# Routing of a mixture-of-experts layer: pair counting and the router's bias moved to TensorE, one put per four tiles, rows combined two tiles ahead

## The chip, the cores and the metric

The kernel runs on one core of a Trainium2 chip. The metric is the device time of one execution in microseconds (us). In the text PE is TensorE (matrix products), PEld its weight loads, DVE is VectorE, ACT is ScalarE, POOL is GpSimd and SP is SyncE, which issues most DMAs. The chip's memory blocks are SBUF (working memory of 128 partitions) and PSUM (where PE writes).

## The reference, cut to what matters

The program is four layers in a row, each adding to `x` (2048 tokens of 512 numbers: 16 tiles of 128 tokens). The change concerns layer 1, a mixture of 32 experts with 4 chosen for each token:

```python
x = x + _L1_ffn_ref(_L1_cond_ref(x, subject, cond_weights), ...)

def _L1_cond_ref(x, subjects, weights):
    w = weights[subjects]
    return jnp.einsum('bct,bcd->bdt', x, w)

def _L1_ffn_ref(hidden_states, gate_w, gate_b, w_gate, b_gate, w_up, b_up, w_down, b_down):
    E, K = 32, 4
    x = hidden_states.reshape(-1, Hh)
    logits = x @ gate_w.T + gate_b
    topk_logits, topk_idx = jax.lax.top_k(logits, K)
    topk_weight = jax.nn.softmax(topk_logits, axis=-1)
    flat_idx = topk_idx.reshape(-1)
    xs = jnp.repeat(x, K, axis=0)
    order = jnp.argsort(flat_idx)          # tokens sorted by expert
    xt = xs[order]
    ...                                    # gate, up, SwiGLU, down: one product per expert
    outs = outs[inv].reshape(-1, K, Hh)
    return jnp.sum(outs * topk_weight[..., None], axis=1)
```

## The kernel before

Each layer is one function. Layer 0 is itself a mixture of experts (7 experts, 2 chosen); its experts' rows lie in a DRAM scratch tensor `ys`, two rows per token. Layer 1 (`layer1`, from L1051) begins by adding these rows to the token stream and choosing its own experts. That is the stage the change touches. It loops over the 16 tiles of 128 tokens, and for tile `i`:

- `combined` (L980 and on, the add on L988): for each of the two choices of layer 0, POOL issues an indirect DMA (a gather, L284) of 128 rows of `ys` into a buffer `yk` (four buffers), and DVE multiplies them with the gate and adds them to the tile: two adds per tile, the second one completes `x`. Its result is kept in `xk` (named `x1in` in the profile).
- `mm` (L1074): PE multiplies with the conditioning weights; ACT copies the result to `c` (L1076, three buffers); SP writes `c` to the DRAM tensor `rows` (L1077).
- `tp` (L1080): PE transposes `c` in four pieces; ACT copies to `cT` (L1082).
- `rp` (L1085): four PE products with the router's weights; DVE adds the bias, giving `lg` (L1087).
- `choose` (L748, in the profile L751 and L752): DVE takes the eight highest of 32 logits and their indices.

After a group of tiles `put` (L754) gives each token-and-expert pair a slot in a table sorted by expert. It is called with groups of 4, 4, 4, 2, 1 and 1 tiles, each one tile behind the choice:

- `chosen` (L758) and `hot` (L761): the indices become a one-hot array of tiles x 4 choices x 32 experts, in f32.
- `sel` (L766) sums the four choices; `pre` (L768) keeps a running sum over tiles, one add per tile.
- `at` (L771, L772): PE multiplies a matrix of ones with `pre` (pairs in earlier tiles, plus the expert's first slot) and a strictly upper triangular matrix with `sel` (pairs of earlier tokens in the tile). The sum is each token's next slot for each expert.
- the product of `hot` and `at` (L773) and its sum `sl` (L775) pick the slot of each pair; six small DVE steps (L777 to L780, L728 to L733) split it in tile and row.
- `mark` (from L723): DVE builds two one-hot arrays `b` and `a` (L737), ACT scales `a` with the token's number (L743), and PE multiplies them (L745) into a table of token numbers by slot, which DVE adds to `tokens` (L746).

`end` (L783) turns `tokens` into the integer list `stok` (L785). The next stage starts with gathers of `rows` by `stok` (`xr`, L284), transposes (L909) and the experts' products (L928, L947).

The loop is written tile by tile, but a scheduler orders each engine's instructions when the kernel is built; each engine then works through its own list in order. What the program says first decides what the scheduler may place early.

Of the kernel before, what the change touches and what calls it, by code (L numbers as in the profile page):

```python
# [9 lines left out]
F32 = mybir.dt.float32  # L10
BF16 = mybir.dt.bfloat16
# [4 lines left out]
ALU = mybir.AluOpType  # L16
AX = mybir.AxisListType
# [3 lines left out]
P = 128  # L21
B, T, D = 32, 64, 512
NT = B * T // P
# [6 lines left out]
E1, K1, C1, V1 = 32, 4, 320, 56  # L30
UNIT = 320
BIG = 65536.0
W0, W1R = 3072, 3076
# [647 lines left out]
class Moe:  # L681
# [4 lines left out]

    def __init__(self, g, ctx, keep, E, K, C, V, wname, wlen, act, scale):
        self.g, self.keep, self.E, self.K, self.C, self.V = g, keep, E, K, C, V  # L690
        self.wname, self.wlen, self.act, self.scale = wname, wlen, act, scale
        tc = g.tc
        self.tiles = E * C // P
        self.rows = g.stream(f"rows{E}")
        self.ys = g.ys[E]
        self.slot = g.const.tile([P, NT, K], I32, name=f"slot{E}")
        self.gates = g.const.tile([P, NT, K], F32, name=f"gates{E}")
        self.vals = keep.tile([P, NT, 8], F32, name=f"vals{E}")
        self.chosen = keep.tile([P, NT, K], F32, name=f"chosen{E}")
        self.place = keep.tile([P, NT, K], F32, name=f"place{E}")  # L700
        self.idx = keep.tile([P, NT, 8], U32, name=f"idx{E}")

        self.pre = keep.tile([P, NT + 1, E], F32, name=f"pre{E}")
        self.count = keep.tile([P, E], F32, name=f"count{E}")
        self.stok = keep.tile([P, self.tiles], I32, name=f"stok{E}")
        self.wp = ctx.enter_context(tc.tile_pool(name=f"ew{E}", bufs=3, reuse_waits="tile"))
        self.wts = {}
# [8 lines left out]
    def begin(self, sb, bank, at):  # L716
        nc, iota = self.g.nc, self.g.c("iota")[:, 0 : self.E]
        self.bank, self.at = bank, at
        nc.vector.tensor_scalar(self.pre[:, 0], iota, self.C / P, None, ALU.mult)
        self.tok = sb.tile([P, self.tiles], F32, name="tokens", bufs=1)  # L720
        nc.vector.memset(self.tok, 0.0)

# [31 lines left out]
    def put(self, sb, i, n):  # L754

        g, nc, E, K, C = self.g, self.g.nc, self.E, self.K, self.C
        fi, place = self.chosen[:, i : i + n, :], self.place[:, i : i + n, :]
        nc.vector.tensor_copy(fi, self.idx[:, i : i + n, 0:K])  # L758
        shape = [P, n, K, E]
        hot = sb.tile(shape, F32, name=f"hot{n}", bufs=1)  # L760
        nc.vector.tensor_tensor(  # L761
            hot, g.c("iota")[:, 0:E].unsqueeze(1).unsqueeze(1).to_broadcast(shape),
            fi.unsqueeze(3).to_broadcast(shape), ALU.is_equal,
        )
        sel = sb.tile([P, n, E], F32, name=f"sel{n}")
        nc.vector.tensor_reduce(sel, hot.rearrange("p n k e -> p n e k"), AX.X, ALU.add)  # L766
        for j in range(n):
            nc.vector.tensor_tensor(self.pre[:, i + j + 1], self.pre[:, i + j], sel[:, j], ALU.add)  # L768

        at = self.at[:, 0 : n * E].rearrange("p (n e) -> p n e", n=n)  # L770
        nc.tensor.matmul(at, g.ones, self.pre[:, i : i + n], start=True, stop=False)  # L771
        nc.tensor.matmul(at, g.c("upper"), sel, start=False, stop=True)  # L772
        nc.vector.tensor_tensor(hot, hot, at.unsqueeze(2).to_broadcast(shape), ALU.mult)  # L773
        sl = sb.tile([P, n, K], F32, name=f"sl{n}")
        nc.vector.tensor_reduce(sl, hot, AX.X, ALU.add)  # L775
        slot = self.slot[:, i : i + n, :]
        nc.vector.tensor_copy(slot, sl)  # L777
        nc.vector.scalar_tensor_tensor(place, fi, -float(C), sl, ALU.mult, ALU.add)
        ov = sb.tile([P, n, K], F32, name=f"ov{n}")
        nc.vector.tensor_scalar(ov, place, float(C), BIG, ALU.is_ge, ALU.mult)  # L780
        self.mark(sb, self.bank[:, 0 : self.tiles], self.tok, sl, slot, ov, i, n, self.tiles)

    def end(self, sb):  # L783
        g, nc, E, C = self.g, self.g.nc, self.E, self.C
        nc.vector.tensor_copy(self.stok, self.tok)  # L785

        lim = sb.tile([P, E], F32, name="lim")
        nc.vector.tensor_scalar(lim, g.c("iota")[:, 0:E], float(C), float(C), ALU.mult, ALU.add)  # L788
        tot = self.at[:, 0:E]
        nc.tensor.matmul(tot, g.ones, self.pre[:, NT], start=True, stop=True)  # L790
        nc.vector.tensor_tensor(self.count, tot, lim, ALU.subtract)
        nc.vector.tensor_scalar(self.count, self.count, 0.0, None, ALU.max)

# [257 lines left out]
def layer1(g, bridge, combined, beside, w2):  # L1051
    tc, nc, a = g.tc, g.nc, g.a
    with ExitStack() as ctx:
        keep = ctx.enter_context(tc.tile_pool(name="l1keep", bufs=1, reuse_waits="tile"))
# [2 lines left out]

        xk = w2["pool"].tile([P, NT, D], F32, name="x1in", tag="sb_mu")
        bd = g.load(keep, "b_d1")
        m = Moe(g, ctx, keep, E1, K1, C1, V1, "w_e1", W1R, l1_expert, None)  # L1060
        with ExitStack() as c1:
            wp = c1.enter_context(tc.tile_pool(name="l1w", bufs=1, reuse_waits="tile"))
            sb = c1.enter_context(tc.tile_pool(name="l1sb", bufs=3, reuse_waits="tile"))
            ps = c1.enter_context(tc.tile_pool(name="l1ps", bufs=2, space=PSUM, reuse_waits="tile"))
            wr = g.load(wp, "w_r1")
            br = g.load_bcast(wp, "b_r1")
            bank, at = (ps.tile([P, 512], F32, name=k, tag=k, bufs=1) for k in ("tok", "at"))
            m.begin(sb, bank, at)

            groups = {3: 4, 7: 4, 11: 4, 13: 2, 14: 1, 15: 1}  # L1070
            for i in range(NT):
                x = combined(sb, i, 3, bridge.x[i], xk[:, i])
                o = ps.tile([P, D], F32, name="mm", tag="mm")
                nc.tensor.matmul(o, bridge.weights[i], x, start=True, stop=True)  # L1074
                c = sb.tile([P, D], F32, name="c")
                nc.scalar.copy(c, o)  # L1076
                nc.sync.dma_start(out=m.rows[i * P : (i + 1) * P, :], in_=c)  # L1077
                tp = ps.tile([P, 4, P], F32, name="tp", tag="tp")
                for cc in range(4):
                    nc.tensor.transpose(tp[:, cc, :], c[:, cc * P : (cc + 1) * P], g.ident)  # L1080
                cT = sb.tile([P, 4, P], F32, name="cT", bufs=2)
                nc.scalar.copy(cT, tp)  # L1082
                rp = ps.tile([P, E1], F32, name="rp", tag="rp")
                for cc in range(4):
                    nc.tensor.matmul(rp, cT[:, cc, :], wr[:, cc, :], start=cc == 0, stop=cc == 3)  # L1085
                lg = sb.tile([P, E1], F32, name="lg")
                nc.vector.tensor_tensor(lg, rp, br, ALU.add)  # L1087
                m.choose(i, lg)
                for last in (i - 1, i) if i == NT - 1 else (i - 1,):
                    if last in groups:  # L1090
                        m.put(sb, last + 1 - groups[last], groups[last])
# [1049 lines left out]
```

## Time and profile before

| | |
|---|---|
| median of the three runs (lowest to highest) | 2775.95 us (2772.17 to 2790.0) |
| the profiled execution: time, span | 2785.32 us, 2783.5 us |
| mean granted TensorE clock | 0.956 of full |
| busy share of the span: PE, PEld, DVE, ACT, POOL | 93%, 59%, 50%, 27%, 30% |
| first gather of the stage, last add, last choice, slot list written | 636.9, 706.9, 714.6, 725.5 us |
| DVE and PE busy within 636.9 to 725.6 | 63.2 and 60.1 of 88.7 us |

The times of the profile run from the span's start. A row of the timeline gives the start, the duration, the engine, the line, the operation with output and inputs, and in brackets how long the engine had been idle and what released it. A duration of DVE overlaps the next one's start by some 0.08 us, since instructions are pipelined. PE's clock is granted by a throttle, in this stage full in some stretches and half in others.

### The profile page before, as it was taken

How to read it: one execution, taken by the hardware profiler on the slowest of the kernel's cores; microseconds unless marked ns; L12 is line 12 of the kernel's file. 1: busy time of each engine (PE TensorE's matmuls, PEld its weight loads, DVE VectorE, ACT ScalarE, POOL GpSimd, SP SyncE). 2: the span in 40 equal slices, each digit the busy share in tenths (PEclk: the TensorE clock that was granted, in tenths of full speed). 3: DMA queues.
4: the chain of work that ended last, by engine and by line, in shares of the span. 5: the costliest groups of instructions: out<-in, count | busy, mean ns of one | idle time of the engine just before them, and what ended most of it. 6: DMA issues, size and time to landing. Idle time of an engine off the chain costs nothing.

```text
span 2783.5 us, 42018 instructions
## 1 busy us (share of the span) xinstructions
PE 2575.4 (93%) x16556; PEld 1641.2 (59%) x16571; DVE 1401.2 (50%) x3479; ACT 749.3 (27%) x1557; POOL 846.4 (30%) x904
## 2 busy tenths in 40 slices
PE   7999979996799999979899999999999999787778
PEld 5777756654455655646666666766666654344444
DVE  4666655735653333335554444555444326465556
ACT  2444421112211121111222222222322212444444
POOL 2222225504212223212222222222222028654550
PEclk9999999997799999998999999999999999888889
DMA  2333224446456865533000000110001034233330
GB/s 95 128 127 128 85 95 155 157 142 193 153 191 238 313 233 190 197 131 113 27 28 27 28 27 31 46 32 27 27 27 50 9 113 145 66 95 89 98 98 29
DMA packets 107076, 291.20 MB, mean 105 GB/s; under 512 B 20681, under 2 KB 21481, under 8 KB 99568
## 3 DMA queue, kind: packets, MB, share of 16 engines
q1 hardware_dynamic: 71232, 193.46, 19.4%
q0 software_dynamic: 35056, 89.13, 10.7%
q10 hardware_dynamic: 576, 5.77, 0.5%
q8 instruction: 135, 2.21, 0.3%
q14 instruction: 77, 0.63, 0.1%
HBM read 216.76 MB, written 87.56 MB: 109 GB/s over the span
## 4 chain that ended last, share of the span: by engine, by line
PE 49%; DVE 2%; issue 2%; another core or an unknown queue 1%; DMA 1%; ACT 1%; POOL 0%; SPq 0%; ACTq 0%; POOLq 0%; DVEq 0%
PE lp L1374 8%; PE out L1517 8%; PE zp L1451 8%; PE pp L1831 3%; PE hp L1483 3%; PE gp L1506 2%; PE y L2078 2%; PE sp L2009 2%; PE yp L1319 2%; PE op L2056 2%; PE pT L2031 2%; PE ep L1460 1%; PE kp L1982 1%; PE ap L1307 1%
## 5 line engine op out<-in xcount | busy, mean ns | idle before, releaser
L928 PE MATMUL gu<-xT,wt 128*128 128x320 f32 x1472 | 407.1, 434 | 0.0
L928 PEld LDWEIGHTS gu<-xT,wt 128*128 128x128 f32 x1472 | 277.6, 191 | 119.5 <-issue 11.3
L1374 PEld LDWEIGHTS lp<-xnT,sb_mu 128*128 128x128 f32 x2048 | 236.3, 194 | 8.6 <-issue 6.7
L1374 PE MATMUL lp<-xnT,sb_mu 128*128 128x128 f32 x2048 | 239.3, 277 | 1.5 <-DVE xnT L256 0.8
L947 PE MATMUL y<-wt,hT 128*128 128x512 f32 (+1 forms) x552 | 238.7, 606 | 0.6 <-DVE yo L256 0.6
L1517 PE MATMUL out<-sb_w,gT 128*128 128x512 f32 x512 | 233.9, 599 | 0.0
L1451 PE MATMUL zp<-sb_w,xnT 128*128 128x512 f32 x512 | 226.5, 592 | 0.0
L1510 DVE COPY gT<-gp 128x512 f32<-128x512 f32 x64 | 44.2, 691 | 235.4 <-PE gp L1506 235.1
L284 POOL DMA_INDIRECT xr<-rows,stok x115 | 110.0, 957 | 154.1 <-PE tp L909 85.3
L1451 PEld LDWEIGHTS zp<-sb_w,xnT 128*128 128x128 f32 x512 | 93.7, 190 | 104.7 <-issue 100.9
L1517 PEld LDWEIGHTS out<-sb_w,gT 128*128 128x128 f32 x512 | 93.5, 190 | 103.8 <-issue 95.4
L947 PEld LDWEIGHTS y<-wt,hT 128*128 128x128 f32 (+1 forms) x552 | 80.0, 171 | 105.5 <-issue 88.4
L677 POOL TENSOR_TENSOR ga<-ga,sg 128x320 f32<-128x320 f32 x64 | 55.2, 862 | 284.2 <-ACT sg L673 283.4
L284 POOL DMA_INDIRECT yk<-ys,slot x96 | 99.0, 1032 | 125.7 <-DVE lim L788 65.4
L2016 DVE CUSTOM_DVE_ANT_0 s<-sp,mask 128x336 f32<-128x336 f32 x128 | 61.2, 503 | 138.5 <-PE sp L2009 40.0
L1528 POOL TENSOR_TENSOR xt<-xt,bc_bias 128x512 f32<-128x512 f32 x16 | 20.3, 1267 | 359.9 <-DMA x<-xt 359.9
L1488 ACT ACTIVATE h<-hp 128x512 f32<-128x512 f32 x128 | 69.5, 594 | 214.2 <-PE hp L1483 214.1
L284 POOL DMA_INDIRECT kvt<-kv,gidx x96 | 93.5, 974 | 107.0 <-PE op L2056 81.9
L1412 POOL TENSOR_TENSOR eT<-eT,inv 128x512 f32<-128x512 f32 x64 | 71.6, 1119 | 152.2 <-DVE inv L1411 151.2
L284 POOL DMA_INDIRECT kvt<-newkv,oidx x96 | 96.5, 1005 | 33.1 <-issue 29.2
L2078 PE MATMUL y<-sb_w_o,oT 128*128 128x512 f32 x128 | 75.8, 677 | 20.3 <-ACT oT L2059 9.2
L2020 ACT ACTIVATE s<-s,m 128x336 f32<-128x336 f32 x128 | 72.9, 572 | 74.5 <-DVE m L2016 53.3
(388 smaller groups left out, 4601.0 us busy)
## 6 DMA issues: line engine op xcount, KB each, us to landing
wt<-w_e SPq DMA_DIRECT2D x32, 1538.0 KB
ys<-yo SPq DMA_DIRECT2D x115, 256.0 KB
ys<-zero SPq DMA_DIRECT2D x10, 2048.0 KB
xt<-x SPq DMA_DIRECT2D x62, 256.0 KB
wt<-w_e SPq DMA_DIRECT2D x7, 1536.0 KB
x<-xt SPq DMA_DIRECT2D x32, 256.0 KB
sb_w<-w SPq DMA_DIRECT2D x5, 1024.0 KB
rows<-hn SPq DMA_DIRECT2D x16, 256.0 KB
```

What stands on the lines that cost most here:

```text
L284: ins = self.nc.gpsimd.indirect_dma_start(out=out, out_offset=None, in_=src, in_offset=bass.IndirectOffsetOnAxis(ap=idx, axis=0), **kw)
L928: nc.tensor.matmul(o, wj[:, c, ic * P : (ic + 1) * P], xT[:, c, :], start=c == 0, stop=c == 3)
L947: nc.tensor.matmul(y[row : row + n, :], hTs[u][:, ic, col : col + n], wd[:, ic, :], start=ic == 0, stop=ic == 1,)
L1374: g.first(e + c, nc.tensor.matmul(lp[:, e, :], w["mu"][:, c, (4 * q + e) * P : (4 * q + e + 1) * P], self.xnT[:, c, :], start=c == 0, stop ...
L1412: g.pin(nc.gpsimd.tensor_tensor(e3, e3, inv.unsqueeze(2).to_broadcast([P, 8, T]), ALU.mult))
L1451: g.first(c, nc.tensor.matmul(zp, self.xnT[:, c, :], w["w1"][:, c, cols], start=c == 0, stop=c == 3))
L1483: g.first(e + b, nc.tensor.matmul(hp[:, b, e, :], self.ews[q][r, e, :], self.z[q][r, e * P : (e + 1) * P], start=True, stop=True))
L1488: g.pin(nc.scalar.activation(self.hs[q][b], hp[:, b], AF.Gelu))
L1517: g.first(e, nc.tensor.matmul(self.out, self.gTs[q][:, e, :], w["w2"][:, 4 * q + e, :], start=q + e == 0, stop=q + e == 6 and q == 3))
L1831: nc.tensor.matmul(pp, xT[i][:, c, :], (w["w_kv3"] if z else wq)[:, c, :], start=c == 0, stop=c == 3)
L2020: nc.scalar.activation(p, p, AF.Exp, bias=m, scale=-1.0, accum_out=tot)
L2078: nc.tensor.matmul(yp, self.oT[i][:, c // 2, c % 2, :], w["w_o3"][:, c, :], start=c == 0, stop=c == 3)
```

## The change

Layer 1's routing object gets a flag `counts`. With it:

- `hot` is written in bf16. `sel` and `pre` are gone. A running count `base` (32 numbers, the same in each partition) starts as each expert's first slot.
- PE adds up the slots in PSUM: `base` through the identity matrix into `n + 1` blocks of 32 columns, then for each of the four choices the upper triangular matrix times `hot` (4 products), then for each tile and choice the matrix of ones times `hot` into all later blocks (16 products). Block `n` holds the count after the group; ACT copies it to `base`.
- The product goes to an array of its own, `own`, in f32. `end` reads the totals from `base`.
- The router's bias is a fifth PE product into `rp` (one row of ones times the bias), and `choose` reads `rp` in PSUM. `lg` is gone, and the bias is loaded as one row.
- `put` is called for groups 4, 4, 4, 4.
- Tile `i + 2` is combined before tile `i` is multiplied (three tiles before the first).

```diff
+        self.base = keep.tile([P, E], F32, name=f"base{E}") if counts else None
+        self.masks = keep.tile([P, 2, P], BF16, name=f"masks{E}") if counts else None
...
+        if self.base is not None:
+            nc.vector.tensor_scalar(self.base, iota, float(self.C), None, ALU.mult)
+            for j, k in enumerate(("upper", "ones")):
+                nc.vector.tensor_copy(self.masks[:, j], self.g.c(k))
...
-        hot = sb.tile(shape, F32, name=f"hot{n}", bufs=1)
+        hot = sb.tile(shape, BF16 if self.base is not None else F32, name=f"hot{n}", bufs=1)
...
+        own = hot
+        if self.base is None:
...
+        else:
+            own = sb.tile(shape, F32, name=f"own{n}", bufs=1)
+            every = self.at[:, 0 : (n + 1) * E].rearrange("p (n e) -> p n e", n=n + 1)
+            at = every[:, 0:n]
+            nc.tensor.matmul(
+                every, g.ident, self.base.unsqueeze(1).to_broadcast([P, n + 1, E]), start=True, stop=False
+            )
+            for k in range(K):
+                nc.tensor.matmul(at, self.masks[:, 0], hot[:, :, k], start=False, stop=False)
+            for j in range(n):
+                for k in range(K):
+                    nc.tensor.matmul(
+                        every[:, j + 1 :], self.masks[:, 1], hot[:, j : j + 1, k].to_broadcast([P, n - j, E]),
+                        start=False, stop=j == n - 1 and k == K - 1,
+                    )
+            nc.scalar.copy(self.base, every[:, n])
+        nc.vector.tensor_tensor(own, hot, at.unsqueeze(2).to_broadcast(shape), ALU.mult)
...
-        nc.vector.tensor_reduce(sl, hot, AX.X, ALU.add)
+        nc.vector.tensor_reduce(sl, own, AX.X, ALU.add)
...
-            br = g.load_bcast(wp, "b_r1")
+            br = g.load(wp, "b_r1")
...
-            groups = {3: 4, 7: 4, 11: 4, 13: 2, 14: 1, 15: 1}
+            groups = {3: 4, 7: 4, 11: 4, 15: 4}
             for i in range(NT):
-                x = combined(sb, i, 3, bridge.x[i], xk[:, i])
+                for j in range(3) if i == 0 else (i + 2,):
+                    if j < NT:
+                        combined(sb, j, 3, bridge.x[j], xk[:, j])
+                x = xk[:, i]
...
-                    nc.tensor.matmul(rp, cT[:, cc, :], wr[:, cc, :], start=cc == 0, stop=cc == 3)
-                lg = sb.tile([P, E1], F32, name="lg")
-                nc.vector.tensor_tensor(lg, rp, br, ALU.add)
-                m.choose(i, lg)
+                    nc.tensor.matmul(rp, cT[:, cc, :], wr[:, cc, :], start=cc == 0, stop=False)
+                nc.tensor.matmul(rp, g.ones[0:1, :], br, start=False, stop=True)
+                m.choose(i, rp)
```

## Prediction

> **What bounds the kernel now.** I read the cores first (one core, span 2783.5 us, mean clock 0.956; the execution's own time is 2785.32 us), then the table by stretches, to find the stage that the change touches: the first gather of layer 1's rows starts at 636.93 us, and the list of token slots (`stok`) is written at 725.34 us. Nothing before or behind is edited. Columns: stretch, its length, busy time of PE, weight load, DVE, ACT, POOL (instructions in brackets), granted clock, DMA share, GB/s.
>
> ```profile
> 640.00:660.00 20.00, 13.98 (x48) 8.16 (x49) 10.07 (x18) 4.10 (x7) 15.73 (x15) 0.67 0.78 243
> 660.00:680.00 20.00, 16.24 (x87) 11.62 (x85) 12.47 (x57) 6.65 (x12) 10.91 (x11) 0.85 0.69 212
> 680.00:700.00 20.00, 15.93 (x96) 11.28 (x96) 18.89 (x48) 8.30 (x16) 5.63 (x5) 0.83 0.48 155
> 700.00:720.00 20.00, 12.66 (x78) 9.75 (x78) 17.89 (x72) 7.02 (x14) 0.00 (x0) 0.59 0.47 184
> 720.00:740.00 20.00, 10.58 (x43) 7.80 (x44) 11.33 (x50) 2.40 (x5) 10.40 (x11) 0.56 0.59 192
> ```
>
> The reader sees two halves. Up to 660 POOL issues gathers nearly without a pause (15.73 of 20 us) and DVE is half idle; from 680 on DVE is the engine that is never free (18.89 and 17.89 of 20 us), while PE falls to a clock of 0.59. The whole kernel is bound by PE elsewhere (93% busy), but here PE is fed through DVE. The waits of 636 to 726 us say who is late:
>
> ```profile
> DVE x1in L988 <- DMA yk<-ys,slot: 10.3, 9, 4.6
> DVE lg L1087 <- PE mm L1074: 6.8, 2, 4.7
> POOL yk L284 <- DVE vals L751: 10.5, 2, 7.7
> ACT c L1076 <- remote: 7.4, 1, 7.4
> DVE hot L773 <- PE at L772: 1.4, 3, 0.7
> ```
>
> DVE waits for gathered rows only at the start; later the gathers wait for DVE (up to 7.7 us), because a `yk` buffer is freed by an add that stands behind routing work. The two other large waits are one event: between 658.0 and 664.2 us DVE, ACT and PE's next step all stand, for which the busy rows show no work. DVE's timeline gives the three marks that I count with, and POOL's the next stage's start:
>
> ```profile
> 662.67 0.19 DVE L1087 TENSOR_TENSOR lg<-rp,bc_b_r 128x32 f32<-128x32 f32 x1 [4.66 <-PE mm L1074]
> ...
> 706.11 0.75 DVE L988 SCALAR_TENSOR_TENSOR x1in<-yk,gates,x1in 128x512 f32<-128x512 f32 x1
> ...
> 714.41 0.19 DVE L752 FIND_INDEX8 idx<-vals,lg 128x8 uint32<-128x32 f32 x1
> ...
> 725.34 0.20 DVE L785 CAST stok<-tokens 128x80 int32<-128x80 f32 x1
> ```
> ```profile
> 726.28 0.94 POOL L284 DMA_INDIRECT xr<-rows,stok  x1 [32.81 <-DVE stok L785]
> ```
>
> So part A ends with the last add, 706.86. Part B, from there to tile 15's choice (714.60), takes 7.7 us. Part C, from the choice to the slots (725.54), takes 10.9 us. The expert weights are issued at 710.2 and land by 724.2, so they don't end last.
>
> **The change, part by part.** DVE's groups of the stage (busy, mean ns, idle before):
>
> ```profile
> L766 DVE TENSOR_REDUCE sel<-hot 128x128 f32<-128x512 f32 x3 | 3.1, 1028 | 0.0
> L1087 DVE TENSOR_TENSOR lg<-rp,bc_b_r 128x32 f32<-128x32 f32 x16 | 2.9, 184 | 11.1 <-PE mm L1074 6.8 <-PE rp L1085 2.5 <-remote 1.3
> L768 DVE TENSOR_TENSOR pre<-pre,sel 128x32 f32<-128x32 f32 x16 | 2.9, 182 | 0.0
> L737 DVE TENSOR_TENSOR b<-sb_cst,row 128x2048 f16<-128x2048 f32 x3 | 6.8, 2283 | 0.0
> L737 DVE TENSOR_TENSOR a<-sb_cst,tl 128x1280 f16<-128x1280 f32 x3 | 4.4, 1482 | 0.0
> ```
>
> *Removed from DVE.* Instructions overlap by some 0.08 us in the timeline (706.01, 706.11 are a `pre` and the next start), so a group's price is the distance to the next start. Ahead of the last add there are in the old order three wide `sel` (3 x 0.94) and one half-wide (0.58 long, 0.49): 3.3 us; 13 `pre` x 0.10: 1.3; 15 `lg` x 0.10: 1.5. The built program's order moves more behind the last add: the product and reduction for tiles 8 to 11 (0.61 + 0.60), `chosen` and `hot` for 12 and 13 (0.06 + 0.32), two choices (2 x 0.27): 2.1. Together 8.2 us less DVE work in part A. DVE is the busy engine in the last 27 us of A, so I count all of it; if it were hidden by waits for PE it would be worth 0, which is the second rival. The new `base` and `masks` writes (between the 0.18 us of a 32-wide row and the 0.69 of a 512-wide one, each) lie in the 4.56 us in which DVE waits for the first gather. Without that cover the three would cost 0.5 to 2.
>
> *Added on PE.* Each put now needs 20 bf16 pairs between `hot` and the product. No row shows their widths (128 down to 32 columns, mean 90). The nearest is the slot count's f16 pair of 80 columns: 12 in 0.75 us with a last one of 0.20 at full clock, 0.05 each; 8 in 0.72 with a last one of 0.27 at half clock, 0.064. Scaled by 90/80: 1.1 to 1.45 us. The upper bound is the f32 transpose of 128 columns, 0.109 and 0.213 a piece: 2.2 to 4.3. I take the f16 rows, same kind of element. [...] Then ACT copies `base` (the 586 ns copies are of 512 columns; this has 32; 0.3 with hand-over, bounds 0.1 and 0.6), and in the built program the product waits for that copy. In the first three puts the order has adds or choices between `hot` and product, so of about 2 us 1.5 is covered: +0.6 over the 1.4 us that DVE waits there now. The bias takes one f32 matmul (two passes of 0.112 or 0.213) per tile behind the router's four: 0.2 to 0.4 us x 16 on PE, which is 50 of 66 us busy in A: inside the next item.
>
> *Rows two tiles ahead.* POOL's order of gathers is unchanged; what moves is DVE's. In the old order 8 or 9 other adds stand between a tile's second add and its `lg` (tiles 0 and 1); in the new one 5 to 7 stand ahead of its maximum (tiles 0 to 4). So a choice may wait with later adds behind it, and with them the gather buffers and POOL's next gathers. Five adds at the pace of the first 19 gathers (661.64 - 636.93 over 18, 1.37 us) are 6.9 us. A tile's chain is, at full and half clock, matmul 1.1 to 2.0, copy 0.6, transposes 0.6 to 1.1, copy 0.6, router and bias 1.3 to 2.4, hand-overs 0.3: 4.5 to 7.0 us, and tiles queue behind each other on PE. I take +1.0 over the present waits; bounds -2 (the rp waits of 2.5 nearly gone) and +10 (rival two).
>
> A: 706.9 - 8.2 + 0.6 + 1.0 = 700.3.
>
> *B.* New order after the last add: product of 8 to 11, choice 13, reduction, choice 14, the small slot steps, `b`, `a`, and only then choice 15. PE must do the counting pairs, tile 13's router, tile 15's matmul and tile 14's router first. Last add to choice 14: pairs and copy 1.6, router 1.1 to 2.1, matmul 1.0 to 1.7, router and end 1.2 to 2.3: 5.2 to 7.8 (full and half clock, with transposes 0.3). Then small steps 0.8, `b` and `a` 2.20 + 1.48, choice 0.4: 10.1 to 12.7. I take 11.0: +3.3.
>
> *C.* One put of four tiles instead of 2, 1, 1. From the choice: `gates`, `chosen`, `hot` 1.0; 20 pairs with 8 slot matmuls of the put before between them 1.45 + 0.5 + 0.25; `base` 0.3; product 0.7, with two small ones 0.2, reduction 0.7; small steps 0.9; `b` and `a` 3.7; four ACT scalings 1.9 (712.30 in the trace shows them behind `a`); last slot matmuls, sum and cast 1.0. Sum 12.6: +1.7. Of the table load for the exponential (1.28 us) I charge nothing: ACT has it done under `hot` and the pairs; without that cover it delays `base` by up to 1.3. PE stands at 0.50 of its clock in all of 706.9 to 725.6 now, so I price C's pairs at half clock; at full clock they would take 0.35 less. [...]
>
> Sum: -8.2 + 0.6 + 1.0 + 3.3 + 1.7 = -1.6 us. From 2785.32 that is 2783.7 for a profiled execution; the median of the runs shown is 2775.95, 9.4 lower, so 2774.3.
>
> **Rivals.** (1) *DVE's relief shows whole and the gathers set the pace.* 32 gathers at 1.37 us: the last starts at 636.93 + 31 x 1.37 = 679.4, lands 4.0 later, add 0.75: A at 684.2; with B 11.0 and C 12.6 the end is 707.8, -17.7 us: 2758. For: POOL's first 19 go at this pace. Against: the new order binds adds to earlier choices. If also the stand of 658 to 664 went (6.2 us), 2752. (2) *PE's chain replaces DVE, slower.* The place is DVE's queue, where a choice stands ahead of the second add two or three tiles later; it decides once A runs at a clock under 0.6 (now 0.78). At half clock PE needs per tile 1.71 + 4 x 0.21 + 10 x 0.21 = 4.65, 16 of them 74, four puts x 2.1: 83 us from 641, so the last choice comes at 724 to 726, and with C the end is near 738: +12, 2788. For: the half-clock rows of B and C, the smaller lead. Against: PE's own extra work keeps the clock up. (3) *The stand of 658 to 664 us moves with the denser gathers*, 6 us either way, within no change.
>
> **How the numbers follow.** About 1% (27.8 us) is what a measurement of this kernel can tell from no change. The forecast, no change at 2774, has 0.72, with its own range 2764 to 2785; rival one 0.17, of which 0.06 passes 1%; rival two 0.11, of which 0.05 does. Low end: no stand -6.2, waits -3.0, B -0.9, run scatter -4 (lowest run against the median): 2760. High end: waits +9, B +1.7, scatter +4: 2789. Faster 0.06, same 0.89, slower 0.05.
>
> **What would show it.** Right: the last add near 700, choice 15 near 711, `stok` near 724, DVE busy in the stage near 53 us instead of 63.2. Rival one: last add before 690 and no POOL wait over 2 us. Rival two: DVE's largest wait is a maximum for the router's bias, and the clock in 640 to 706 under 0.6. I am wrong if the stage moves by over 15 us, or if time moves outside it.

## The result, and the profile after

The changed kernel takes 2784.12 us (median of 12 runs, 2781.82 to 2789.76), the kernel before 2776.30 (12 runs beside them, 2767.08 to 2790.0). The ratio is 1.0029, 95% interval [1.0015, 1.0043]: slower by about 8 us, where 1.6 us of gain were forecast. The median lies inside the forecast's range of 2760 to 2789, but the move goes the other way.

The profiled execution of the changed kernel has a span of 2786.8 us. Its table by stretches, in the columns of the one shown before (busy time of PE, weight load, DVE, ACT, POOL, then granted clock, DMA share, GB/s):

```profile
640.00:660.00 20.00, 8.85 (x30) 4.78 (x30) 7.64 (x14) 2.34 (x4) 13.67 (x14) 0.65 0.64 180
660.00:680.00 20.00, 17.12 (x89) 12.46 (x88) 8.42 (x24) 5.76 (x10) 11.30 (x12) 0.74 0.69 205
680.00:700.00 20.00, 18.35 (x128) 13.65 (x127) 15.12 (x47) 7.46 (x16) 8.21 (x8) 0.91 0.53 173
700.00:720.00 20.00, 16.71 (x109) 12.33 (x108) 13.54 (x35) 7.00 (x14) 0.96 (x1) 0.80 0.37 116
720.00:740.00 20.00, 6.56 (x60) 5.38 (x59) 13.77 (x44) 5.56 (x11) 3.66 (x4) 0.59 0.57 228
```

This execution reached its first gather at 642.4 us, 5.4 later than the one before (the work ahead of it is not edited; over all profiles that mark lies between 636.9 and 645.2), so the rows are compared by what lies inside the stage. DVE was the engine that was never free (18.89 and 17.89 of 20 us); now it is busy for 15.12 and 13.54, and PE has taken its place with 17.12, 18.35 and 16.71. The marks, from DVE's timeline:

```profile
710.85 0.74 DVE L1017 SCALAR_TENSOR_TENSOR x1in<-yk,gates,x1in 128x512 f32<-128x512 f32 x1
...
721.83 0.19 DVE L759 FIND_INDEX8 idx<-vals,rp 128x8 uint32<-128x32 f32 x1
...
734.48 0.20 DVE L811 CAST stok<-tokens 128x80 int32<-128x80 f32 x1
```

Part A (first gather to the end of the last add) is 69.2 us (before 69.9), part B (to tile 15's choice) 10.4 (7.7), part C (to the slot list) 12.7 (10.9). From the first gather to the first expert product it is 101.6 us against 98.0. So these two executions differ by 3.8 us up to the slot list, and by 3.3 in their spans, while the medians differ by 7.8: the profiled execution of before lies 9 us above its median, that of the change 4.5. No profile here says where the other 4 us lie. What DVE waited for from 636 to 726 us (in total, times, longest):

```profile
DVE x1in L1017 <- DMA yk<-ys,slot: 11.0, 6, 7.0
DVE vals L758 <- remote: 5.8, 1, 5.8
DVE vals L758 <- PE rp L1118: 5.7, 6, 1.5
DVE tokens L753 <- PE tok L752: 3.7, 3, 1.3
DVE own L799 <- ACT base L798: 3.0, 2, 1.9
DVE vals L758 <- issue: 2.7, 1, 2.7
```

L1118 is the new bias product: DVE's choices (`vals`) now wait for PE. The totals of part A, from the busy time of each engine in that stretch, before and after:

```profile
636.90:706.80 69.90, 49.55 (x257) 33.83 (x257) 47.87 (x145) 20.64 (x38) 34.73 (x32) 0.77 0.57 179
```
```profile
642.40:711.60 69.20, 53.35 (x291) 36.92 (x292) 39.98 (x102) 19.80 (x38) 34.10 (x32) 0.77 0.59 176
```

DVE works 47.87 - 39.98 = 7.9 us less in A, and A is only 0.7 us shorter. The mean clock of A is the same, 0.77. Where the other 7.2 us went is the question of the experiments.

### The profile page after: what moved, and what is told of

The parts are those of the page before. It is cut to its first block, busy times and chain, and to the rows that moved or that the text cites. A ratio compares the mean times of both kernels' runs of the same rounds, so it can differ in the third digit from the quotient of the medians.

```text
span 2786.8 us, 42147 instructions
## 1 busy us (share of the span) xinstructions
PE 2583.7 (93%) x16650; PEld 1649.4 (59%) x16665; DVE 1395.6 (50%) x3416; ACT 749.4 (27%) x1561; POOL 844.2 (30%) x904
## 4 chain that ended last, share of the span: by engine, by line
PE 49%; DVE 2%; issue 2%; another core or an unknown queue 1%; DMA 1%; ACT 1%; POOL 0%; POOLq 0%; ACTq 0%; SPq 0%; DVEq 0%
PE lp L1405 8%; PE out L1548 8%; PE zp L1482 8%; PE pp L1862 3%; PE hp L1514 3%; PE gp L1537 2%; PE y L2109 2%; PE sp L2040 2%; PE pT L2062 2%; PE op L2087 2%; PE yp L1350 2%; PE ep L1491 1%; PE kp L2013 1%; PE ap L1338 1%
## 5 line engine op out<-in xcount | busy, mean ns | idle before, releaser
L284 POOL DMA_INDIRECT yk<-ys,slot x96 | 98.1, 1022 | 129.4 <-SPq L845 66.1
L938 PEld LDWEIGHTS tp<-sb_cst,xr 128*128 128x128 f32 x460 | 53.5, 147 | 66.3 <-issue 32.9
```

Of the source, the lines that this page charges most:

```text
L284: ins = self.nc.gpsimd.indirect_dma_start(out=out, out_offset=None, in_=src, in_offset=bass.IndirectOffsetOnAxis(ap=idx, axis=0), **kw)
```

## The experiments

Two kinds of comparison are used. The time is the median and the ratio to the kernel before, run beside it on the same chip. A, B and C are from one profiled execution each. In some sets of runs the kernel before takes about 2680 us, in the others 2771 to 2779 (the record has both for the chip that it numbers 1); in the sets of 2680, A is some 3 to 7 us shorter for the same kernel (66.4 against 69.2 for the changed one), so A is compared among sets of the same level only. "vs before" in us is the median of before times the ratio less one; it need not be the difference of the medians (for "changed, no bias" -6.7 against -2.1).

| kernel | median (before) | ratio [95%] | vs before, us | A, B, C | clock in A |
|---|---|---|---|---|---|
| before, shown / once more | - | - | - | 69.9, 7.7, 10.9 / 69.8, 7.7, 11.0 | 0.77 / 0.74 |
| changed kernel | 2784.12 (2776.30) | 1.0029 [1.0015, 1.0043] | +8.1 | 69.2, 10.4, 12.7 | 0.77 |
| look only | 2681.88 (2679.77) | 1.0005 [0.9993, 1.0017] | +1.3 | 64.9, 6.6, 14.8 | 0.74 |
| counts only | 2677.79 (2679.77) | 0.9991 [0.9983, 1.0000] | -2.4 | 59.7, 10.0, 7.4 | 0.84 |
| bias only | 2691.95 (2679.77) | 1.0048 [1.0034, 1.0062] | +12.9 | 65.4, 14.2, 12.0 | 0.79 |
| groups only | 2682.32 (2679.77) | 1.0003 [0.9991, 1.0015] | +0.8 | 60.5, 6.2, 16.9 | 0.84 |
| bias copied | 2792.05 (2778.83) | 1.0049 [1.0030, 1.0067] | +13.6 | 79.6, 12.1, 12.8 | 0.61 |
| PSUM, no bias | 2786.10 (2778.83) | 1.0032 [1.0013, 1.0052] | +8.9 | 70.1, 12.3, 11.2 | 0.72 |
| changed, bias on DVE | 2773.14 (2778.83) | 0.9984 [0.9966, 1.0002] | -4.4 | 67.9, 10.0, 12.7 | 0.70 |
| changed, no bias | 2769.04 (2771.17) | 0.9976 [0.9961, 0.9992] | -6.7 | 63.8, 9.7, 12.7 | 0.77 |
| changed, ring | 2781.16 (2771.17) | 1.0047 [1.0032, 1.0062] | +13.0 | 62.3, 22.1, 12.0 | 0.76 |
| changed, bias twice | 2774.78 (2771.17) | 1.0011 [0.9995, 1.0028] | +3.0 | 72.9, 10.9, 12.7 | 0.71 |
| counts and look | 2767.93 (2771.17) | 0.9994 [0.9975, 1.0012] | -1.7 | 64.5, 10.8, 9.8 | 0.74 |
| changed, again | 2685.06 (2681.27) | 1.0014 [1.0005, 1.0023] | +3.8 | 66.4, 9.9, 12.7 | 0.72 |
| changed, no bias, again | 2675.77 (2681.27) | 0.9976 [0.9967, 0.9985] | -6.4 | 57.1, 9.8, 12.7 | 0.80 |
| changed, bias in one pass | 2675.01 (2681.27) | 0.9975 [0.9966, 0.9984] | -6.7 | 57.6, 9.6, 12.7 | 0.80 |
| changed, bias twice, again | 2686.49 (2681.27) | 1.0011 [1.0003, 1.0020] | +2.9 | 69.3, 10.8, 12.7 | 0.72 |
| changed, wide scores | 2779.03 (2775.55) | 1.0001 [0.9982, 1.0021] | +0.3 | 60.9, 17.7, 11.7 | 0.78 |
| one pass, wide | 2771.42 (2775.55) | 0.9986 [0.9966, 1.0005] | -3.9 | 59.3, 13.6, 12.6 | 0.81 |

### One part at a time, on the kernel before

Look only: the adds run two tiles ahead. Counts only: the flag `counts`. Bias only: the bias product and the choice from `rp`. Groups only: the last put of four.

```diff
+                for j in range(3) if i == 0 else (i + 2,):          # look only
+                    if j < NT:
+                        combined(sb, j, 3, bridge.x[j], xk[:, j])
...
+        m = Moe(g, ctx, keep, E1, K1, C1, V1, "w_e1", W1R, l1_expert, None, True)   # counts only
...
+                nc.tensor.matmul(rp, g.ones[0:1, :], br, start=False, stop=True)   # bias only
+                m.choose(i, rp)
...
+            groups = {3: 4, 7: 4, 11: 4, 15: 4}                      # groups only
```

> The kernel before with one part of the change: rows combined two tiles ahead. Theory 1 (order): putting each choice closer behind its tile's adds makes DVE wait for PE's chain with later adds behind it; this part alone costs +4 to +10 us. Theory 2 (PE and ACT in DVE's path): the counting on PE with its copy of the base costs the time; this part alone is within -3 to +2 us. Theory 3 (the end of the stage): only the last put of four tiles costs; this part alone within -3 to +2 us.

> The kernel before with one part of the change: pairs counted on PE (bf16 one-hots, base copied by ACT), groups of 4, 4, 4, 2, 1, 1, bias on DVE, rows not ahead. Theory 1: DVE's relief of sel and pre (5 us) shows, -6 to 0 us. Theory 2: the product now waits for 20 matmuls and ACT's copy six times, +3 to +8 us, with DVE's waits for base over 5 us in sum. Theory 3: -5 to 0 us.

> The kernel before with one part of the change: the router's bias as a fifth product into PSUM, the maximum read from PSUM. Theory 1: -3 to +1 us (1.6 us of DVE gone). Theory 2: 0 to +3 us, since each router chain is 0.2 to 0.4 us longer on PE. Theory 3: -3 to +1 us.

> The kernel before with one part of the change: the last four tiles in one put instead of 2, 1, 1. Theory 3: +3 to +6 us, from the last choice to the slot list about 12.5 us instead of 10.9. Theories 1 and 2: 0 to +2 us.

None of the three parts that the theories on record name (the order of the rows, counting, the last put) moves the time by more than 2.4 us. Counting as the cost is excluded by its interval; for the order (up to +4.6 us) and the last put (up to +4.0, with a C of 16.9 where 12.5 was expected) the intervals just reach the low ends of what was expected. The part that none of them named, the bias, costs 12.9 us by itself.

### Which half of the bias part costs: the product, or reading PSUM twice

The kernel before is profiled once more here, for its A, B and C on another chip. In "bias copied" the bias is added on PE and DVE copies the sum out of PSUM at once, so a bank is as short-lived as before. In "PSUM, no bias" the bias is left out and the choice reads PSUM, so the bank is held as in the change. In "changed, bias on DVE" only the bias part of the change is undone.

```diff
-                m.choose(i, rp)                       # bias copied, from bias only
+                lg = sb.tile([P, E1], F32, name="lg")
+                nc.vector.tensor_copy(lg, rp)
+                m.choose(i, lg)
...
-                nc.tensor.matmul(rp, g.ones[0:1, :], br, start=False, stop=True)   # PSUM, no bias
...
-                m.choose(i, rp)                       # changed, bias on DVE
+                lg = sb.tile([P, E1], F32, name="lg")
+                nc.vector.tensor_tensor(lg, rp, br, ALU.add)
+                m.choose(i, lg)
```

> The kernel before itself, profiled on the chip of the experiments (one look). Expected, if the bias part's cost of about 13 us sits in the stage between the first gather of rows and the first expert product: a stage shorter than the 100.8 us of the bias-only kernel by 8 to 13 us, so 88 to 93. If the cost sits elsewhere (layer 2, or the stage of layer 0): a stage of 97 to 101 us, and the rest of the kernel shorter than the 1947.6 us of the bias-only kernel.

> Before with the bias added on TensorE, and the sum then copied from PSUM to SBUF by VectorE, which chooses from the copy: VectorE has as many instructions as before, TensorE has the extra product, and the PSUM bank of a tile's scores is free again after one short copy. Theory 'held bank' (the bias part costs because the choice reads PSUM twice, and the next-but-one tile's router product waits for the second read): no change against before, -3 to +3 us. Theory 'TensorE's extra product' (the K=1 product lengthens the router's chain): as slow as the bias-only kernel, +8 to +13 us.

> Before with no bias added at all (left out: the router's bias), the choice made straight from PSUM: no extra product on TensorE, no add on VectorE, and the bank held through Max and MaxIndex. Theory 'held bank': about as slow as the bias-only kernel, +8 to +13 us. Theory 'TensorE's extra product': faster than before by up to VectorE's 16 adds of 0.2 to 0.3 us, -5 to 0 us.

> The changed kernel with only the bias back on VectorE (added there on the way out of PSUM, as before): counts on TensorE, groups of four, rows combined two tiles ahead. If the bias part alone turned the change into a loss: faster than before by 2 to 8 us, the stage 5 us or more shorter than the changed kernel's 101.6. If the parts only lose together (order and the last put of four): within 2 us of before or slower, stage 98 us or more.

The look at before does not place the cost: its stage is 97.7 us, as in the profile shown (98.0), but the 100.8 us of "bias only" that it was to be held against come from a set of the other level. Of the two theories neither stands alone: both halves cost, each +8.9 us or more. But the order of DVE's instructions in these two kernels also differs from the order before in thirty to forty places, so what the order did is not kept apart. The product's half is seen in "bias copied", first in what DVE waits for, then in the busy time of A (before, once more, below it):

```profile
DVE lg L1117 <- PE rp L1115: 22.9, 10, 6.4
```
```profile
643.90:723.50 79.60, 62.72 (x252) 43.85 (x253) 44.06 (x126) 19.34 (x35) 37.57 (x32) 0.61 0.49 153
```
```profile
645.20:715.00 69.80, 49.11 (x257) 33.37 (x257) 48.13 (x145) 20.61 (x38) 34.05 (x32) 0.74 0.57 179
```

PE is busy for 62.72 us instead of 49.11 and its clock falls from 0.74 to 0.61; A is 9.8 us longer. The other half lies in B. In "PSUM, no bias" A stays (70.1), but tile 15's index (L759) stands behind the wide `b` and `a`, though its maximum was taken at 715.80:

```profile
715.80 0.20 DVE L758 MAX8 vals<-rp 128x8 f32<-128x32 f32 x1 [0.59 <-PE rp L1114]
...
716.70 2.29 DVE L744 TENSOR_TENSOR b<-sb_cst,row 128x2048 f16<-128x2048 f32 x1
718.90 1.48 DVE L744 TENSOR_TENSOR a<-sb_cst,tl 128x1280 f16<-128x1280 f32 x1
...
720.70 0.19 DVE L759 FIND_INDEX8 idx<-vals,rp 128x8 uint32<-128x32 f32 x1
```

So B is 12.3 instead of 7.7: an order that the scheduler built. In the whole change that place was priced in part B of the forecast. With the bias back on DVE the change has a median 5.7 us below before, though its interval just reaches 1. Its second mark was missed: its stage was to be 5 us or more shorter than the changed kernel's 101.6 and is 99.9, longer than the 97.7 of before on the same chip. So this run does not show that the bias alone turned the change into a loss.

### Nothing, one, or twice the product, in the changed kernel

```diff
-                nc.tensor.matmul(rp, g.ones[0:1, :], br, start=False, stop=True)   # no bias: left out
...
+                nc.tensor.matmul(rp, g.ones[0:1, :], br, start=False, stop=False)  # bias twice: one more
...
-                rp = ps.tile([P, E1], F32, name="rp", tag="rp")                    # ring
+                rp = ring[:, i % 4, 0:E1]           # ring: one tile [P, 4, P] in PSUM, bufs=1
...
-            groups = {3: 4, 7: 4, 11: 4, 15: 4}                                    # counts and look:
+            groups = {3: 4, 7: 4, 11: 4, 13: 2, 14: 1, 15: 1}                      # and the bias on DVE
```

> The changed kernel without any bias (left out: the router's bias), the choice still straight from PSUM. VectorE's order is the changed kernel's but for a few neighbours; TensorE loses 32 passes of 0.297 us, 9.5 us in all. Theory 'TensorE's extra product' (TensorE is nearly fully busy for about 30 us of the stage, so what is added there lengthens it): 5 to 10 us faster than the changed kernel, about 0 to -3 us against before. Theory 'held bank' (what costs is the PSUM bank held through Max and MaxIndex): as slow as the changed kernel, +5 to +10 us against before.

> The changed kernel with the router's scores of four tiles in four parts of one PSUM bank instead of two banks: the bias product stays on TensorE, and a router product no longer waits for a choice two tiles back. Theory 'held bank': -5 to +1 us against before. Theory 'TensorE's extra product': as the changed kernel, +5 to +10 us.

> The changed kernel with the bias product made twice (the bias is then added twice). Another 32 passes of 0.297 us on TensorE. Theory 'TensorE's extra product': 6 to 10 us more than the changed kernel, +13 to +18 us against before. Theory 'held bank': TensorE has room, +6 to +10 us against before, no more than the changed kernel.

> Counts on TensorE and rows combined two tiles ahead, the bias added by VectorE as before, and the last puts of two, one and one tile as before: the changed kernel without the two parts that gained nothing or lost. Expected: faster than before, -3 to -9 us; if the put of four is what the look-ahead needs to pay, -2 to +3 us.

Without any bias the change is faster than before by 6.7 us (2.1 by the medians), at an order on DVE that differs in the place of one add and two maxima beside it. The busy time of its A:

```profile
639.70:703.50 63.80, 46.91 (x265) 32.06 (x266) 40.14 (x102) 20.01 (x38) 33.80 (x32) 0.77 0.62 191
```

DVE's 40.14 us are the change's 39.98; PE has 46.91 instead of 53.35, and A is 5.4 us shorter. This is against the theory of the held bank: here too the choice reads PSUM twice. (The expectations speak of 9.5 us for the product's 32 passes; their rows overlap, and by the group of L1118 in the changed kernel, 6.9 us of PE, 297 ns a pass, they are fewer.)

```profile
L1118 PE MATMUL rp<-sb_b_r,sb_cst 1*128 1x32 f32 x32 | 6.9, 297 | 0.0
```

The ring did not do what it was for. Its PE rows show the router's product waiting for the index of the choice before it, so the four parts of one tile were not free of each other:

```profile
716.50 1.91 PE L1118 MATMUL rp<-sb_w_r,cT 128*128 128x32 f32 x8 [0.22 <-DVE idx L759]
...
723.21 1.46 PE L1118 MATMUL rp<-sb_w_r,cT 128*128 128x32 f32 x6 [4.24 <-DVE idx L759]
```

It tells nothing of the held bank, and its +13.0 us lie outside what either theory had. "Bias twice" went against both theories: by that of the product it should have been 13 to 18 us slower than before, by that of the held bank 6 to 10, and it was 3.0. "Counts and look" is no different from before; 3 to 9 us of gain were expected, or -2 to +3 if the look-ahead needs the put of four to pay.

### Four doses on one chip

The bias in one pass is split into three bf16 rows whose sum has about the precision of f32, on partitions 0, 32 and 64 of a zeroed array; one bf16 product over 96 rows adds them.

```diff
+            br = g.load_bcast(wp, "b_r1")
+            ...                                     # b3: rows 0, 32, 64 = br and what bf16 left of it
-                nc.tensor.matmul(rp, g.ones[0:1, :], br, start=False, stop=True)
+                nc.tensor.matmul(rp, m.masks[0:96, 1], b3[0:96, :], start=False, stop=True)
```

> The changed kernel itself, beside the three others of this call: two f32 passes a tile for the bias (about 9.5 us of TensorE). Theory 'TensorE's extra product': +5 to +10 us against before, above the kernel without the bias by 6 to 12 us. Theory 'order' (the time follows the order in which VectorE's adds and choices were placed, and TensorE's load does not matter): within 3 us of the kernel without the bias, whose order is the same but for one add.

> The changed kernel without any bias (left out: the router's bias), once more: no pass for the bias. Theory 'TensorE's extra product': -2 to -7 us against before. Theory 'order': as the changed kernel, within 3 us.

> The changed kernel with the bias split into three bf16 rows and added by one bf16 pass over 96 rows: one pass a tile, about 4 us of TensorE, and VectorE's order in the stage is exactly that of the kernel without the bias. Theory 'TensorE's extra product': between the two, 2 to 5 us above the kernel without the bias, -3 to +3 us against before. Theory 'order': as the kernel without the bias, within 2 us.

> The changed kernel with the bias product made twice (the bias is then added twice), once more beside the others: four f32 passes a tile, about 19 us of TensorE; VectorE's order differs from the changed kernel's in some ten places. Theory 'TensorE's extra product': 6 to 12 us above the changed kernel. Theory 'order': anything between the kernel without the bias and the changed kernel, as the first look at it (+3 us against before) has it.

By medians: none 2675.77, one bf16 pass 2675.01, two f32 passes 2685.06, four 2686.49. That is a step, no slope: one bf16 pass costs nothing, two f32 passes cost 9.3 us, two more 1.4. The theory of the product had a price for every pass and fails at one pass and at four; that of the order fails at two. The profiles of none and of two f32 passes agree with the step: 88.7 against 98.1 us from the first gather to the first expert product. Their parts A (two f32 passes, then none):

```profile
637.60:704.00 66.40, 55.82 (x294) 40.08 (x295) 40.20 (x102) 20.61 (x39) 32.54 (x32) 0.72 0.60 184
```
```profile
638.60:695.70 57.10, 43.97 (x265) 30.45 (x266) 39.79 (x102) 20.14 (x38) 35.76 (x32) 0.80 0.70 214
```

PE is busy 11.9 us longer, more than the 5.9 us of the passes' own rows in A (26 rows, 310 ns each), and at a lower clock, 0.72 against 0.80. Following the ends of the adds from the first gather, the two executions are together at the 20th (34.2 and 34.3 us), 2.9 us apart at the 21st, 8.0 at the 24th and 9.3 at the last. The 20th add is also the one whose place in DVE's order differs; behind the maxima, indices and slot steps beside it the two orders are the same, and 6.4 of the 9.3 us open there. What lies there in the change (DVE's timeline):

```profile
673.21 0.20 DVE L758 MAX8 vals<-rp 128x8 f32<-128x32 f32 x1 [1.10 <-PE rp L1118]
...
674.55 0.20 DVE L758 MAX8 vals<-rp 128x8 f32<-128x32 f32 x1 [1.07 <-PE rp L1118]
...
686.75 0.24 DVE L753 TENSOR_TENSOR tokens<-tokens,tok 128x80 f32<-128x80 f32 x1 [4.93 <-PE tok L752]
```

and what PE did meanwhile:

```profile
671.86 0.97 PE L1117 MATMUL rp<-sb_w_r,cT 128*128 128x32 f32 x8
672.77 0.40 PE L1118 MATMUL rp<-sb_b_r,sb_cst 1*128 1x32 f32 x2
673.10 1.08 PE L1117 MATMUL rp<-sb_w_r,cT 128*128 128x32 f32 x8
674.11 0.40 PE L1118 MATMUL rp<-sb_b_r,sb_cst 1*128 1x32 f32 x2
...
677.11 1.75 PE L1117 MATMUL rp<-sb_w_r,cT 128*128 128x32 f32 x8
678.80 0.63 PE L1118 MATMUL rp<-sb_b_r,sb_cst 1*128 1x32 f32 x2
...
681.20 1.92 PE L1117 MATMUL rp<-sb_w_r,cT 128*128 128x32 f32 x8 [0.73 <-ACT cT L1114]
683.05 0.63 PE L1118 MATMUL rp<-sb_b_r,sb_cst 1*128 1x32 f32 x2
```

The same eight passes take 0.97 us at 671.86 and 1.75 to 1.92 from 677 on. The granted clock of the stretches goes with it (of the change, then of the kernel without the product in the last one):

```profile
671.70:675.10 3.40, 3.40 (x26) 3.07 (x25) 1.23 (x11) 0.78 (x2) 0.94 (x1) 1.00 0.78 249
675.10:688.70 13.60, 12.87 (x70) 9.91 (x69) 8.62 (x17) 4.34 (x9) 4.29 (x4) 0.50 0.33 103
```
```profile
675.10:688.70 13.60, 10.44 (x92) 7.90 (x90) 12.66 (x35) 6.20 (x12) 7.74 (x7) 1.00 0.67 211
```

PE is busy in all of 671.7 to 675.1 at full clock, and then for 13.6 us gets half of it. Without the product it has the full clock in all of these 13.6 us. So in this pair the step goes with the clock, and the question is why it fell behind a stretch in which PE was busy throughout. The pair of the first level (the changed kernel of the result, and "changed, no bias") is less clear: there the mean clock of A is 0.77 in both, the fall behind a busy stretch lasts 3.4 us, and the gap opens in small steps, 2.6 us by the 19th add, 4.6 by the 21st and 5.4 at the last. How much of these 5.4 us is the clock and how much the passes' own time is not shown.

### What the clock follows

In every profile the clock changes only at the ends of stretches of 3.413 us (in the kernel before, the times at one clock that end between 636 and 738 us last 3.413 to 34.133 us, each a whole number of such stretches). For the full-clock stretches between 636 and 745 us of the 20 profiles I counted what PE's rows show in them: the busy share, and the columns that passes streamed (a pass is one matrix instruction of PE; in the rows above the four f32 products of the router stand as x8, two passes each; the four f32 transposes of a tile stand as x4, one each). A pass counts with its columns (32 for the router, 512 for `mm`), twice that if it is f32, and by its part at an edge.

```
after the stretch        how many   columns streamed   busy share
the clock fell to half       85       0 to 3006         up to 1.00 (nine of them at 1.00)
the clock stayed full       195    3062 and more        0.44 and more
```

No stretch is an exception. By the busy share alone, at the threshold that fits best, 34 of the 280 would stand on the wrong side; of the 115 that were busy throughout, the nine that fell streamed 2269 to 3006 and the 106 that stayed 3525 and more. (At half clock the line is not as sharp: the lowest count after which the full clock came back is 2978, the highest after which it did not is 3628.) The change's stretch of 671.7 streamed 2968 by this count, and that of 661.4 2994: 16 router and 4 bias passes, which are 1280 of them, take 2.6 us of it. From start to start, a bias pass takes 0.17 us for 32 columns there and a pass of `mm` 0.43 for 512. All nine falls behind a fully busy stretch are in kernels with the f32 product: the changed kernel (three in two profiles), bias copied (two) and bias twice (four in two); kernels without it have none, and neither have three others with it (bias only, ring, wide scores). A count that leaves out the bias passes, or weighs each pass by its rows (1 of 128 there), parts the stretches just as well (2858 and 3062), so whether these passes count at all is open.

The last two kernels raise the columns alone: all router and bias passes write 128 columns, the 32 four times.

```diff
-                    nc.tensor.matmul(rp, cT[:, cc, :], wr[:, cc, :], start=cc == 0, stop=False)
+                    nc.tensor.matmul(rpw, cT[:, cc, :], wr[:, cc : cc + 1, :].to_broadcast([P, 4, E1]),
+                                     start=cc == 0, stop=False)
```

> The changed kernel with every pass of the router's product and of the bias made 128 columns wide instead of 32 (the 32 columns repeated four times; the choice reads the first 32): the same 10 passes a tile, four times the columns streamed, nothing gained in the result. VectorE's order shifts in some places. Theory 'columns' (the granted clock of a 3.4 us stretch follows the columns that TensorE streamed in the stretch before, not the time in which it was busy; the bias passes cost because they take time and stream few columns, and the clock halves): the clock of the stage's first part rises from 0.72 to 0.9 or more, the first part shortens to 55 to 60 us from 66.4, and the kernel takes -3 to -10 us against before. Theory 'time of the passes' (what the passes add is their own time): wider passes take longer, the clock stays near 0.72, +4 to +12 us against before.

> The kernel with the bias in one bf16 pass, its router and bias passes made 128 columns wide in the same way. Theory 'columns': the clock of the first part rises from 0.80 to 0.9 or more; as that kernel was hardly held by TensorE any more, a further 0 to 4 us, -6 to -11 us against before. Theory 'time of the passes': some 3 to 6 us more than with 32 columns, -3 to 0 us against before.

Both theories missed their numbers for the time, and "columns" those for the clock and for A too; the clock did as "columns" has it in one respect: the six falls of the two kernels come after stretches with a busy share of 0, 0.07, 0.09, 0.21, 0.49 and 0, none after a busy one. The wide kernel's stretches that begin at 671.9 and 675.4 us are as busy as the changed kernel's of 671.7, with the same kinds of products, but stream 6720 and 6842 columns, and the clock stays full. But the 0.9 was missed (0.78 and 0.81), since PE still stands twice for over 3 us, and the time is not the 3 to 10 us below before: +0.3 [-5.0, +5.8]. A is 60.9, shorter than in both profiles of the changed kernel, but B is 17.7, so A and B together are 78.6 against 79.6: DVE's order moved with the wider passes, and the choices of the last tiles now come behind the last add. This test agrees with the count by columns and shows no gain. Widening the one-pass kernel gained nothing beyond its noise (-3.9 [-9.4, +1.4] against before, -6.7 with narrow passes).

## Why the prediction was wrong, step by step

- **DVE's relief in A, -8.2: right as work.** DVE is busy 7.9 us less in A. In the whole stage it is busy for 54.7 us, forecast near 53.
- **The bias product, "inside the next item": this step failed.** It was costed at 0.2 to 0.4 us a tile (by the rows' starts it takes 0.33 at full clock and 0.57 at half) and then at nothing, since PE was "50 of 66 us busy". Average room was taken for room at the place. Where the router's backlog is worked off, PE had little: it is busy for 52.2 of the 60 us from 660 to 720, and in some stretches throughout. Taking the product out of the changed kernel shortens A by 5.4 us (69.2 to 63.8) and by 9.3 (66.4 to 57.1) in the set of the other level, and there the time by 9.3. Without it A is 6.1 us shorter than before (63.8 against 69.9), where the sum, with the product at nothing, had 6.6.
- **Choices waiting, +1.0, with +10 as the bound.** This is the term in which the 5.4 us turned up: DVE's waits for PE. DVE is idle for 29.2 us of A, 22.0 before and 23.7 in the changed kernel without a bias. The bound held, the value did not. The first forecast mark shows it: the last add was to come 63 us after the first gather and came 69.2 after.
- **B, +3.3 and C, +1.7: right.** Measured +2.7 and +1.8 in the profiles shown. The choice of tile 15 stands behind `b` and `a`, as worked out.
- **The price of the last put of four, and counting on PE.** Neither the counting pairs nor the put cost anything clear of noise by themselves (-2.4 [-4.6, 0] and +0.8 [-2.4, +4.0] us).
- **Rival two** named the place and came near the amount (+12, DVE waiting for a maximum), but its condition, a clock under 0.6 in A, did not come: 0.77. Nor was the maximum behind the bias DVE's largest wait (5.7 us in sum, for gathered rows 11.0), so its nearness is in part luck. Where the clock did fall with the product (0.72 against 0.80 in the second pair), 13.6 us in the middle of A went with most of the loss; it need not fall for all of A. Its argument against itself, "PE's own extra work keeps the clock up", goes with the forecast's table (a clock of 0.56 where PE is busy for 10.58 of 20 us, 0.85 where it is busy for 16.24), but did not hold there: the extra work was narrow passes, and behind the 3.4 us from 671.7, in which PE was busy throughout and streamed 2968 columns by the count, the clock was 0.50.
- **Rival one** has the direction of the change without its bias, at a third of the size (-6.7 instead of -17.7). Its A of 47.3 us is not reached (63.8 and 57.1), though in the second of these DVE's largest wait is then the one for gathered rows, 17.9 us in sum.

What stays open: why the second pair of passes costs only 1.4 us. Its kernel has another order on DVE in some ten places, and its two profiles have A longer by 2.9 and 3.7 us than the change's, so cost and order are not told apart. That few columns cause the fall is supported by the counts and by the wide kernel, where no fall came behind a busy stretch; it is one profile, and the order on DVE moved with it. That the fall makes up all of the 9.3 us is argued from the rows, since the order on DVE also differs in the place of one add and the maxima beside it. The kernel with one pass has the order of the one without a bias (but for seven small steps at the start), and its time: for one pass, nothing is left to the order. It differs from the two f32 passes in element and rows as well as in number, so which of these spares the time is not told apart.

**A version that beats both, by a quarter of a percent:** the change with the bias in one bf16 pass, 2675.01 us against 2681.27 before and 2685.06 for the change on the same chip, ratio 0.9975 [0.9966, 0.9984].

## What to carry to other kernels

Work that is moved to an engine with room on average must be placed against its share in the stretch where it falls; the average over the stage hid that PE was nearly always busy in its middle (18.35 of the 20 us from 680 in the changed kernel). Small products are dear in two ways here. A router pass of 32 columns takes as long as a transpose pass of 128 (0.11 us from start to start at full clock). And where many of them followed each other few columns were streamed (2968 in the 3.4 us from 671.7, by the count above), and the clock was 0.50 for the 13.6 us behind. One bf16 pass with more rows (pieces of the f32 row) in place of two f32 passes took the cost away (2675.01 against 2685.06 us). And a small edit moves the scheduler's order: two kernels differ only in what was edited if the order that was built is the same too, which has to be looked at.

## What the hardware showed that was not expected

In the 280 full-clock stretches of 3.413 us of these profiles the granted clock goes with columns, not with busy time: it fell to half behind each of the 85 with 3006 columns or fewer (f32 twice) and stayed full behind each of the 195 with 3062 or more, about what three f32 passes of 512 count (3072). The f32 transposes are in the count; without them 21 of the 280 stand on the wrong side.

In this stage ACT took up a product 4.95 us after its rows' end. While the gathers run (DMA share 0.64 and 0.69 in the first two stretches shown), in the changed kernel the four transposes of 656.11 are recorded as ended at 656.71, but ACT, free since 658.66, starts the copy of that `tp` at 661.66, after 2.99 us idle; and DVE's maximum at 666.75 has waited 5.85 us for a release that the profile can't name:

```profile
656.11 0.60 PE L1112 MATMUL tp<-sb_cst,c 128*128 128x128 f32 x4
```
```profile
661.66 0.58 ACT L1114 COPY cT<-tp 128x512 f32<-128x512 f32 x1 [2.99 <-PE mm L1106]
```
```profile
666.75 0.49 DVE L758 MAX8 vals<-rp 128x8 f32<-128x32 f32 x2 [5.85 <-remote]
```

A like stand is in the kernel before at 658 to 664 us, where the `lg` of 662.67 had waited 4.66 us. The ends of PE's rows are modelled, so the profile doesn't tell whether the products ended late or their end was seen late. The cause was not tried.
